# The last group's recurrence in a decoder's third layer: keys read from PSUM, own buffers, four passes on GpSimd, VectorE's order by hand

## The chip, the core and the metric

The kernel runs on one core of a Trainium2 chip. The metric is the device time of one execution in microseconds (us); the median of several runs counts. A core has five engines that each follow a queue of their own: TensorE (PE), VectorE (DVE), ScalarE (ACT), GpSimd (POOL) and SyncE (SP), which here issues the DMA transfers.

## The reference, cut to what matters

A decoder of four layers is computed, each with self-attention, attention to a context and a feed-forward part, with a layer norm after each of them. x is 64 sequences of 64 tokens with 256 channels, in float32. The change lies in the second of the three parts of the third layer, in which the context's rows are the values v and x's own rows are the keys k of a recurrence over the tokens:

```python
def step(carry, kv_t):
    p, q, o = carry
    kt, vt = kv_t
    no = jnp.maximum(o, u + kt)
    A = jnp.exp(o - no)
    E = jnp.exp(u + kt - no)
    y = (A * p + E * vt) / (A * q + E)
    no2 = jnp.maximum(w + o, kt)
    A2 = jnp.exp(w + o - no2)
    E2 = jnp.exp(kt - no2)
    return ((A2 * p + E2 * vt, A2 * q + E2, no2), y)
...
x = _layernorm(x + _L2_xattn_ref(64, 64, 256, L2_xattn_w, L2_xattn_u, x, ctx_2048), axis=-1)
x = _layernorm(x + _L2_ffn_ref(x, L2_ffn_weight, L2_ffn_bias), axis=-1)
```

w and u have one value for each of the 256 channels. The part that follows (`_L2_ffn_ref`) quantizes x to FP8 with one scale for the whole of x, so it needs the largest absolute value of all 64 sequences before it can begin.

## The kernel before

The 4096 tokens are eight groups of 512 (`self.X[g]`, here x0 to x7); all of them stay in SBUF, and so does the context, turned (`self.CT[g]`). `l2_mix` does the self-attention and feed-forward of the third layer and the recurrence. Its feed-forward runs over 64 slots, eight for each group (`hidden`, `down`). Beside the slots of a group stand the parts of the next group's attention (`mixing`) and the parts of the recurrence of the group before (`behind`).

`recurrence(g)` splits the 256 channels into two halves c of 128, which lie on the partitions, with the 512 tokens along the columns. The parts of a half:

- `keys`: x[g] is turned on PE (`turned`, four transposes into a PSUM bank) and ScalarE copies it to the tile `k` (L1458).
- `maximum`: a scan on VectorE gives o (L1574).
- `factors`: two passes on VectorE and a memset fill the first two of the four rows of blocks of the tile e (`es[c]`, named l2x_e0 and l2x_e1 or, without numbers, l2x_e); on ScalarE two Relu passes (L1588, L1589) and one Exp over all 2048 columns (L1590) make the four factors.
- `sums`: the values times two of the factors (`ev`, L1593), and two scans (`pq`, L1599).
- `outputs` (L1602, L1605, L1606) and `divided` (a reciprocal, L1609, and a product, L1610): y.

`finish` turns y back on PE (tile yx, L1621), adds x (L1624), normalizes (`normalized`: statistics on VectorE, L331 and L334; the power -1/2 on GpSimd, L305; four passes on ScalarE, L363) and takes the largest absolute value (`linear.largest`, L60). The two halves share one buffer each of o, pq and ev.

What orders the work: PE's order is that of the program (`manual_schedule`); that of the other engines, and of SP's queue, is made by a scheduler of the language from its own estimates. Each queue is worked off in order.

For the last group no slots are left. PE is given filler instead: `fill(n)` computes n of the 28 units of `ContextRows`, keys and values of the fourth layer for some rows of the context. One unit is two matmuls of 128x512 into a PSUM bank (tag kv, three banks, L168), a copy by ScalarE to a buffer in SBUF (L172, four buffers) and a store to DRAM by SP (L173). The end of `l2_mix`:

```python
fill(2)
self.l3a_qk = [self.big_weight(name) for name in ("l3a_wq", "l3a_wk")]
for k, (_, part) in enumerate(behind):
    if k == len(behind) - 1:
        fill(17)
    part()
```

The tiles e0 and e1 are two of the eight slots of the ring in which weights lie. After the recurrence, `l3_attn` begins with `linear.first` (the FP8 part for x0, with the last seven units) and loads l3a_wv and l3a_wproj (L402), two slots each. The second half of l3a_wv takes e0's slot and the first half of l3a_wproj takes e1's, so these loads wait for the last reader of e0 and e1. ScalarE scales l3a_wproj when it has landed (L2008).

Of the kernel before, what the change touches and what calls it, by code (L numbers as in the profile page):

```python
# [10 lines left out]
F32 = mybir.dt.float32  # L11
# [3 lines left out]
AF = mybir.ActivationFunctionType  # L15
ALU = mybir.AluOpType
# [3 lines left out]
P = 128  # L20
# [3 lines left out]
NTOK = TG * P  # L24
# [7 lines left out]
class Linear:  # L32
# [26 lines left out]
    def largest(self, g):  # L59
        self.nc.vector.tensor_reduce(  # L60
            self.cols[:, g : g + 1], self.dec.X[g], AX.XY, ALU.max, apply_absolute_value=True
        )
# [80 lines left out]
class ContextRows:  # L143
# [16 lines left out]
    def fill(self, n, pool, tag, bufs, banks, copy):  # L160

        dec = self.dec
        while n and self.units:
            n -= 1
            g, t, i = self.units.pop(0)
            ps = dec.bank("kv", bufs=banks)
            for c in range(2):
                dec.nc.tensor.matmul(  # L168
                    ps, dec.CT[g][:, c, t * P : (t + 1) * P], self.w[:, i, c, :], start=c == 0, stop=c == 1
                )  # L170
            out = pool.tile([P, 512], F32, tag=tag, name="kv", bufs=bufs)
            copy(out, ps)  # L172
            dec.nc.sync.dma_start(out=self.dram[g, t, i], in_=out)  # L173
# [97 lines left out]
class Decoder:  # L271
# [1145 lines left out]
    def l2_mix(self, ctx, linear):  # L1417
# [8 lines left out]
        nc, ins = self.nc, self.ins  # L1426
        EPS, HC, NB = 1.1920929e-07, 8, NTOK // S
        wk = self.pool(ctx, "l2m", 2)
# [3 lines left out]
        for c in range(2):  # L1432
            w = self.weight(f"l2_wsg{c}")
# [9 lines left out]
        fill = lambda n: context.fill(n, wk, "hid", 4, 3, nc.scalar.copy)  # L1443
        w, u = self.column("l2_w", 2), self.column("l2_u", 2)
        decay = wk.tile([P, 2, NB, S], F32, tag="decay", name="decay", bufs=1)
# [3 lines left out]
        state = {}  # L1449

        def bank(name):
            return self.bank(name, tag="a", bufs=3)

        def turned(src, out, c):
            ps = bank("tr")
            for t in range(TG):
                nc.tensor.transpose(ps[:, t * P : (t + 1) * P], src[:, t, c * P : (c + 1) * P], self.ident)
            nc.scalar.copy(out, ps)  # L1458

# [94 lines left out]
        def recurrence(g):  # L1556


            x, v = self.X[g], self.CT[g]
            k = wk.tile([P, 2, NTOK], F32, tag="k", name="k", bufs=1)  # L1560
            y = wk.tile([P, 2, NTOK], F32, tag="yx", name="yx", bufs=1)
            halves = []
            for c in range(2):
                e = es[c]
                o = wk.tile([P, NTOK + 1], F32, tag="o", name="o", bufs=1)
                pq = wk.tile([P, 2, NTOK + 1], F32, tag="pq", name="pq", bufs=1)
                ev = wk.tile([P, 2, NTOK], F32, tag="ev", name="ev", bufs=1)

                def keys(c=c):
                    turned(x, k[:, c, :], c)  # L1570

                def maximum(c=c, o=o):
                    nc.gpsimd.memset(o[:, 0:1], NEG_INF)
                    nc.vector.tensor_tensor_scan(  # L1574
                        o[:, 1:], decay[:, c].rearrange("p b t -> p (b t)"), k[:, c, :], 0.0, ALU.add, ALU.max
                    )

                def factors(c=c, o=o, e=e):


                    nc.vector.scalar_tensor_tensor(
                        e[:, 0, :], o[:, :NTOK], u[:, c : c + 1], k[:, c, :], ALU.subtract, ALU.subtract
                    )
                    nc.vector.scalar_tensor_tensor(
                        e[:, 1, :], o[:, :NTOK], w[:, c : c + 1], k[:, c, :], ALU.add, ALU.subtract
                    )
                    nc.vector.memset(e[:, 0:2, :].rearrange("p i (b t) -> p i b t", b=NB)[:, :, :, 0:1], NEG_INF)
                    nc.scalar.activation(e[:, 2:4, :], e[:, 0:2, :], AF.Relu)  # L1588
                    nc.scalar.activation(e[:, 0:2, :], e[:, 0:2, :], AF.Relu, scale=-1.0)  # L1589
                    nc.scalar.activation(e, e, AF.Exp, scale=-1.0)  # L1590

                def sums(c=c, e=e, ev=ev, pq=pq):
                    nc.vector.tensor_tensor(  # L1593
                        ev, e[:, 2:4, :], v[:, c, :].unsqueeze(1).broadcast_to([P, 2, NTOK]), ALU.mult
                    )

                    nc.gpsimd.memset(pq[:, :, 0:1], 0.0)
                    for i, add in enumerate((ev[:, 1, :], e[:, 3, :])):
                        nc.vector.tensor_tensor_scan(pq[:, i, 1:], e[:, 1, :], add, 0.0, ALU.mult, ALU.add)  # L1599

                def outputs(e=e, ev=ev, pq=pq):
                    nc.vector.tensor_tensor(  # L1602
                        pq[:, :, :NTOK], pq[:, :, :NTOK], e[:, 0, :].unsqueeze(1).broadcast_to([P, 2, NTOK]), ALU.mult
                    )
                    nc.vector.tensor_tensor(pq[:, 0, :NTOK], pq[:, 0, :NTOK], ev[:, 0, :], ALU.add)  # L1605
                    nc.vector.tensor_tensor(pq[:, 1, :NTOK], pq[:, 1, :NTOK], e[:, 2, :], ALU.add)  # L1606

                def divided(c=c, pq=pq):
                    nc.vector.reciprocal(pq[:, 1, :NTOK], pq[:, 1, :NTOK])  # L1609
                    nc.vector.tensor_tensor(y[:, c, :], pq[:, 0, :NTOK], pq[:, 1, :NTOK], ALU.mult)  # L1610

                halves.append(([keys], [maximum, factors], [sums, outputs, divided]))

            def finish():
                z = wk.tile([P, TG, D], F32, tag="z", name="z")
                for i in range(2):
                    ps = bank("yx")
                    for j in range(2):
                        for c in range(2):
                            at = (2 * i + j) * P  # L1620
                            nc.tensor.transpose(  # L1621
                                ps[:, j * D + c * P : j * D + (c + 1) * P], y[:, c, at : at + P], self.ident
                            )
                    nc.vector.tensor_tensor(  # L1624
                        z[:, 2 * i : 2 * i + 2, :], ps.rearrange("p (t d) -> p t d", t=2), x[:, 2 * i : 2 * i + 2, :], ALU.add
                    )
                self.normalized(x, z)
                linear.largest(g)

            steps = [part for parts in zip(*halves) for half in parts for part in half]  # L1630
            return steps + [lambda: None, finish]

        def mixing(g):

            def two(t):
                qkv(g, t)
                mixed(g, t - 1)

            return [
                lambda: start(g), lambda: qkv(g, 0), lambda: two(1), lambda: two(2), lambda: two(3),  # L1640
                lambda: mixed(g, 3), lambda: None, lambda: outputs_turned(g),
            ]

        with self.tc.manual_schedule(engines={mybir.EngineType.PE}):
            for part in mixing(0):
                part()
            slots = [(g, i) for g in range(self.n_groups) for i in range(HC)]
            parts, behind, done = [], [], []
            for n in range(len(slots) + 2):
                if n < len(slots):  # L1650
                    g, i = slots[n]
                    if i == 0:
                        parts = mixing(g + 1) if g + 1 < self.n_groups else []
                    hidden(g, i)
                if n >= 2:
                    down(*slots[n - 2])
                    if slots[n - 2][1] == HC - 1:
                        behind += [(n + 2, part) for part in recurrence(slots[n - 2][0])]

                        if slots[n - 2][0] == self.n_groups - 2:  # L1660
                            behind[-1] = (len(slots) + 1, behind[-1][1])
                if n == len(slots) + 1:
                    fill(2)

                for _ in range(2 if n < len(slots) - HC else 3):
                    if behind and n >= behind[0][0]:
                        behind.pop(0)[1]()
                if parts:
                    parts.pop(0)()
            fill(2)  # L1670
            self.l3a_qk = [self.big_weight(name) for name in ("l3a_wq", "l3a_wk")]
            for k, (_, part) in enumerate(behind):
                if k == len(behind) - 1:
                    fill(17)
                part()

    def head_rms(self, wk, ps, out, eps, tag):

# [769 lines left out]
```

## Time and profile before

| | |
|---|---|
| median of 5 runs (lowest to highest) | 4342.58 us (4339.46 to 4348.26) |
| profiled execution: its own time, its span | 4344.71 us, 4343.0 us |
| PE busy | 4081.9 us (94%) |
| VectorE busy | 3093.3 us (71%) |
| ScalarE busy | 2018.8 us (46%) |
| GpSimd busy | 1498.6 us (35%) |
| `l2_mix` and the start of `l3_attn` | about 1354 to 1926 us of the span |
| last group's recurrence, first scan to last product of y | 1871.88 to 1902.52 us |

All times in the text are counted from the start of the span, on one profiled execution. A line such as L1574 is a line of the kernel before; where an operation is in a helper, its line is the helper's. Engines are named as in the profile: PE (matmuls; PEld loads weights beside them), DVE, ACT, POOL, SP. "busy" is the share of the span in which an engine computes; the number in brackets at the end of a timeline's line is the idle time before it and what ended it.

### The profile page before, as it was taken

Reading aid. Unit: us, or ns where it says so; the run is one execution under the profiler, and the core shown is the slowest. Engines: PE = TensorE matmul, PEld = TensorE weight load, DVE = VectorE, ACT = ScalarE, POOL = GpSimd, SP = SyncE. Lnnn points to the kernel's source line nnn. Section 1 sums busy time; section 2 is a strip of 40 time slices with the busy share of each in tenths; the row PEclk is TensorE's granted clock in tenths of the full one; section 3 lists DMA queues with packets and bytes.
Section 4 is the critical chain, followed back from the end, with each engine's and each line's share of the span. In section 5 each row is a group of like instructions: output and inputs, shape, how many; then the busy total and the mean of one; then the engine's idle time right before and its main releaser. Section 6 shows DMA issues by size and latency. Waiting matters only on the chain. (4 is left out here: it accounts for less than half of the span.)

```text
span 4343.0 us, 74101 instructions
## 1 busy us (share of the span) xinstructions
PE 4081.9 (94%) x28808; PEld 2636.8 (61%) x28808; DVE 3093.3 (71%) x6211; ACT 2018.8 (46%) x3695; POOL 1498.6 (35%) x1529
## 2 busy tenths in 40 slices
PE   8889999989988999989999999999989999999898
PEld 6645556666665555546666666666656666666566
DVE  6744548888665687877777777777767778787676
ACT  5555535666523566544444444444432333232443
POOL 4411111332431111115555555555533444433111
PEclk9989998999999999999999999999999999999999
DMA  2200012333200000031111111111130000000000
GB/s 84 66 21 10 1 34 64 76 78 70 73 1 12 1 1 1 10 131 26 29 26 28 28 25 30 25 28 27 30 105 20 20 23 23 23 23 13 9 15 16
DMA packets 108295, 144.01 MB, mean 33 GB/s; under 512 B 15844, under 2 KB 73380, under 8 KB 106536
## 3 DMA queue, kind: packets, MB, share of 16 engines
q1 hardware_dynamic: 107944, 139.27, 12.6%
q8 instruction: 228, 3.74, 0.4%
q14 instruction: 123, 1.01, 0.1%
HBM read 70.25 MB, written 26.76 MB: 22 GB/s over the span
## 5 line engine op out<-in xcount | busy, mean ns | idle before, releaser
L305 POOL TENSOR_TENSOR hrq<-hrq,neg_half 128x4 f32<-128x4 f32 x256 | 258.5, 1010 | 570.9 <-DVE hrq L303 568.5
L305 POOL TENSOR_TENSOR rstd<-rstd,neg_half 128x4 f32<-128x4 f32 (+1 forms) x171 | 149.3, 874 | 706.1 <-DVE rstd L303 638.4
L1188 DVE TENSOR_REDUCE mc<-sq 128x2 f32<-128x512 f32 x512 | 317.6, 683 | 67.5 <-PE sk L1186 66.3
L1194 ACT ACTIVATE e<-sk 128x512 f32<-128x512 f32 x512 | 265.8, 608 | 116.4 <-PE sk L1186 114.5
L1183 PE MATMUL sq<-l1x 32*128 32x256 f32 x2048 | 279.2, 412 | 4.9 <-DVE z L1069 3.1
L1186 PE MATMUL sk<-l1x 32*128 32x256 f32 x2048 | 257.3, 398 | 0.0
L1703 PE MATMUL p<-l3a_wq,xt 128*128 128x512 f32 x512 | 242.1, 595 | 11.2 <-DVE v L292 9.9
L305 POOL TENSOR_TENSOR hrk<-hrk,neg_half 128x4 f32<-128x4 f32 x160 | 188.5, 1178 | 178.3 <-DVE hrk L303 173.7
L1703 PE MATMUL p<-l3a_wk,xt 128*128 128x512 f32 x512 | 247.4, 606 | 0.6 <-ACT q L290 0.6
L1183 PEld LDWEIGHTS sq<-l1x 32*128 32x128 f32 x2048 | 211.6, 198 | 58.8 <-issue 23.2
L1703 PE MATMUL p<-l3x_wq,xt 128*128 128x512 f32 x512 | 242.8, 597 | 0.7 <-DVE k L2087 0.7
L2189 PE MATMUL acc<-l3x_wo,yt 128*128 128x256 f32 x1024 | 235.6, 383 | 2.5 <-ACT yt L290 1.2
L1703 PE MATMUL p<-l3a_wv,xt 128*128 128x512 f32 x512 | 234.0, 599 | 0.4 <-ACT y L94 0.4
L1985 PE MATMUL acc<-l3a_wproj,yt 128*128 128x256 f32 x1024 | 232.7, 380 | 0.2 <-DVE yt L292 0.2
L1985 PEld LDWEIGHTS acc<-l3a_wproj,yt 128*128 128x128 f32 x1024 | 194.6, 191 | 53.6 <-issue 29.2
L2063 ACT ACTIVATE sq<-q 128x512 f32<-128x512 f32 x128 | 80.7, 630 | 311.5 <-DVE q L2087 304.2
L2189 PEld LDWEIGHTS acc<-l3x_wo,yt 128*128 128x128 f32 x1024 | 193.1, 192 | 35.5 <-issue 7.4
L1186 PEld LDWEIGHTS sk<-l1x 32*128 32x128 f32 x2048 | 192.1, 190 | 6.8 <-issue 2.9
L311 PEld LDWEIGHTS qT<-ident,q 128*128 128x128 f32 x1024 | 121.5, 141 | 122.0 <-issue 79.8
L311 PE MATMUL qT<-ident,q 128*128 128x128 f32 x1024 | 158.3, 277 | 26.9 <-DVE qT L292 19.7
L1969 POOL TENSOR_TENSOR hry<-hry,neg_half 128x8 f32<-128x8 f32 x64 | 106.3, 1660 | 183.2 <-DVE hry L1965 183.2
L1222 PE MATMUL ret<-e,vt 128*32 128x256 f32 x2048 | 140.4, 389 | 17.4 <-DVE mc L1188 16.4
(401 smaller groups left out, 10205.9 us busy)
## 6 DMA issues: line engine op xcount, KB each, us to landing
vs<-v SPq DMA_DIRECT2D x320, 128.0 KB
l3x_kv<-kv SPq DMA_DIRECT2D x28, 256.0 KB
x<-in_x SPq DMA_DIRECT2D x8, 512.0 KB
ct<-in_ctxT SPq DMA_DIRECT2D x8, 512.0 KB
cn<-in_ctx SPq DMA_DIRECT2D x8, 512.0 KB
l1x<-in_ctx SPq DMA_DIRECT2D x128, 32.0 KB
l1x_x<-x SPq DMA_DIRECT2D x8, 512.0 KB
l1x<-l1x_x SPq DMA_DIRECT2D x128, 32.0 KB
```

Source lines behind the costliest of these rows:

```text
L305: nc.gpsimd.tensor_tensor(out, out, self.neg_half[:, :n], ALU.pow)
L311: self.nc.tensor.transpose(ps[:, j * P : (j + 1) * P], blk, self.ident)
L1183: nc.tensor.matmul(ps[:, n, :], x_[rows, j, part], c_[rows, j, :], start=True, stop=True)
L1186: nc.tensor.matmul(ps[:, n, :], c_[rows, j, part], x_[rows, j, :], start=True, stop=True)
L1188: nc.vector.tensor_reduce(mc[new % 2][:, ra + k, 2 * j : 2 * j + 2], ps, AX.X, ALU.max, negate=True)
L1194: nc.scalar.activation(es[rb + k], ps, AF.Exp, scale=scale)
L1222: nc.tensor.matmul(ret[32 * r : 32 * r + 32, :], vt[i % 2][:, lc, 4 * r + j, :], es[r][:, lc, :], start=lc == 0, stop=lc == 1,)
L1703: self.nc.tensor.matmul(ps, lhs(c), w(c, cols), start=c == 0, stop=c == 1 and bias is None)
L1969: nc.gpsimd.tensor_tensor(r, r, self.neg_half[:, :8], ALU.pow)
L1985: nc.tensor.matmul(acc[:, :D], yts[h % 2][:, h // 2, :], wp[n // 8][:, (n % 8) * D : (n % 8 + 1) * D], start=n == 0, stop=n == 15,)
L2063: nc.scalar.activation(sq, x, AF.Square)
L2189: nc.tensor.matmul(acc[:, :D], yts[h % 2][:, h // 2, :], w.o[n // 8][:, (n % 8) * D : (n % 8 + 1) * D], start=n == 0, stop=n == 15,)
```

## The change

For the last group alone (`last`):

- The scan and the two passes of `factors` read the turned keys from the PSUM banks, without the copy to `k`. `turned` returns the bank when no tile is given.
- Half 1 has its own buffers for `pq` and `ev`: those of the tags xt and k.
- GpSimd does `ev` of half 1 and the three passes of `outputs` of half 0.
- ScalarE does the Exp in two passes of 1024 columns for each half, that of the last two blocks first.
- At the last slot a one-column Exp is put on ScalarE.
- Where VectorE's order before was the scheduler's, it is the program's from the end of the slots on (`manual_schedule` with DVE): the passes that normalize x6 (`apply`) and its maximum (`largest`) are put between the parts of the last recurrence, and half 1 is divided ahead of half 0.
- Three units of filler stand ahead of x6's transposes and one behind, for two and two; fill(17) stands behind the two halves' factors in the program, which in PE's order is behind the turned keys, as before.

For all groups pq is 512 columns wide, the scans have 511 columns, and of the two sums in `outputs` that of the divisor comes first. GpSimd's and ScalarE's order and SP's queue are still the scheduler's. In the built program SP's queue is changed in two places: the load into e0's slot stands behind the store of the sixth unit (it was the eleventh) and the load into e1's slot behind that of the twelfth (it was the sixteenth); on ScalarE the scaling of the first half of l3a_wproj stands behind the copy of unit 15 (it was the nineteenth).

```diff
@@ turned
             for t in range(TG):
                 nc.tensor.transpose(ps[:, t * P : (t + 1) * P], src[:, t, c * P : (c + 1) * P], self.ident)
+            if out is None:
+                return ps
             nc.scalar.copy(out, ps)
+            return out
@@ recurrence
             x, v = self.X[g], self.CT[g]
-            k = wk.tile([P, 2, NTOK], F32, tag="k", name="k", bufs=1)
+            last = g == self.n_groups - 1
+            ks = {}
+            if not last:
+                k = wk.tile([P, 2, NTOK], F32, tag="k", name="k", bufs=1)
...
-                pq = wk.tile([P, 2, NTOK + 1], F32, tag="pq", name="pq", bufs=1)
-                ev = wk.tile([P, 2, NTOK], F32, tag="ev", name="ev", bufs=1)
+                own = last and c == 1
+                pq = wk.tile([P, 2, NTOK], F32, tag="xt" if own else "pq", name="pq", bufs=2 if own else 1)
+                ev = wk.tile([P, 2, NTOK], F32, tag="k" if own else "ev", name="ev", bufs=1)
 
                 def keys(c=c):
-                    turned(x, k[:, c, :], c)
+                    ks[c] = turned(x, None if last else k[:, c, :], c)
...
                     nc.scalar.activation(e[:, 2:4, :], e[:, 0:2, :], AF.Relu)
+                    if last:
+                        nc.scalar.activation(e[:, 2:4, :], e[:, 2:4, :], AF.Exp, scale=-1.0)
                     nc.scalar.activation(e[:, 0:2, :], e[:, 0:2, :], AF.Relu, scale=-1.0)
-                    nc.scalar.activation(e, e, AF.Exp, scale=-1.0)
+                    rest = e[:, 0:2, :] if last else e
+                    nc.scalar.activation(rest, rest, AF.Exp, scale=-1.0)
 
                 def sums(c=c, e=e, ev=ev, pq=pq):
-                    nc.vector.tensor_tensor(
+                    eng = nc.gpsimd if last and c == 1 else nc.vector
+                    eng.tensor_tensor(
                         ev, e[:, 2:4, :], v[:, c, :].unsqueeze(1).broadcast_to([P, 2, NTOK]), ALU.mult
                     )
...
-                        nc.vector.tensor_tensor_scan(pq[:, i, 1:], e[:, 1, :], add, 0.0, ALU.mult, ALU.add)
+                        nc.vector.tensor_tensor_scan(
+                            pq[:, i, 1:], e[:, 1, : NTOK - 1], add[:, : NTOK - 1], 0.0, ALU.mult, ALU.add
+                        )
...
+                def outputs(c=c, e=e, ev=ev, pq=pq):
+                    eng = nc.gpsimd if last and c == 0 else nc.vector
+                    eng.tensor_tensor(
+                        pq, pq, e[:, 0, :].unsqueeze(1).broadcast_to([P, 2, NTOK]), ALU.mult
                     )
-                    nc.vector.tensor_tensor(pq[:, 0, :NTOK], pq[:, 0, :NTOK], ev[:, 0, :], ALU.add)
-                    nc.vector.tensor_tensor(pq[:, 1, :NTOK], pq[:, 1, :NTOK], e[:, 2, :], ALU.add)
+                    eng.tensor_tensor(pq[:, 1, :], pq[:, 1, :], e[:, 2, :], ALU.add)
+                    eng.tensor_tensor(pq[:, 0, :], pq[:, 0, :], ev[:, 0, :], ALU.add)
...
@@ the end of l2_mix
+                if n == len(slots) - 1:
+                    h = state[slots[n][0], "h", slots[n][1]]
+                    nc.scalar.activation(self.small(1, "none", bufs=1), h[:, 0:1], AF.Exp, scale=0.0)
...
-            fill(2)
+            ended(part for _, part in behind)
+
+        with self.tc.manual_schedule(engines={mybir.EngineType.PE, mybir.EngineType.DVE}):
+            fill(3)
+            statistics, apply, largest = before()
+            statistics()
+            fill(1)
             self.l3a_qk = [self.big_weight(name) for name in ("l3a_wq", "l3a_wk")]
-            for k, (_, part) in enumerate(behind):
-                if k == len(behind) - 1:
-                    fill(17)
-                part()
+            (keys0, keys1, *factors, sums0, outputs0, divided0, sums1, outputs1, divided1), finish = recurrence(
+                self.n_groups - 1
+            )
+            keys0()
+            keys1()
+            ended(factors)
+            fill(17)
+            sums0()
+            outputs0()
+            apply()
+            sums1()
+            outputs1()
+            largest()
+            divided1()
+            divided0()
+            ended(finish())
```

## The prediction

> **What bounds the kernel now.** The page first: PE is busy 94% of the span and its row of 40 slices has no hole, so a change on another engine pays only where PE waits. Then the four engines' timelines from 1820 us, where the last group's recurrence lies. All times are the trace's, in us from the span's start; columns are start, duration, engine, line, what is written from what, count, and in brackets the idle time before and who ended it. PE:
>
> ```profile
> 1868.54 10.46 PE L168 MATMUL kv<-l3x_wkv,ct 128*128 128x512 f32 x24
> 1883.27 20.85 PE L168 MATMUL kv<-l3x_wkv,ct 128*128 128x512 f32 x44 [4.26 <-ACT kv L172]
> 1903.95 1.04 PE L1621 MATMUL yx<-ident,yx 128*128 128x128 f32 x8
> ```
>
> These are the 17 filler units (4 records each). A unit takes 1.72 us (the copies of its result follow each other at 1890.46, 1892.18, 1893.89). Units are numbered here 1 to 28 from the first filler; fill(17) is 5 to 21. The transposes of y stand behind them in PE's order and start at 1903.95. VectorE and ScalarE:
>
> ```profile
> 1871.88 1.22 DVE L1574 TENSOR_TENSOR_SCAN o<-decay,k 128x512 f32<-128x512 f32 x1
> ...
> 1881.83 1.23 DVE L1593 TENSOR_TENSOR ev<-l2x_e,ct 128x1024 f32<-128x1024 f32 x1 [4.34 <-ACT l2x_e L1590]
> ...
> 1887.21 0.69 DVE L1606 TENSOR_TENSOR pq<-pq,l2x_e 128x512 f32<-128x512 f32 x1
> ...
> 1901.83 0.69 DVE L1610 TENSOR_TENSOR yx<-pq 128x512 f32<-128x512 f32 x1
> 1904.59 1.29 DVE L1624 TENSOR_TENSOR z<-yx,x 128x512 f32<-128x512 f32 x2 [2.07 <-PE yx L1621]
> ```
>
> ```profile
> 1878.59 1.28 ACT L1590 ACT_TABLE_LOAD   x1
> ...
> 1905.12 2.00 ACT L2008 ACTIVATE l3a_wproj<-l3a_wproj,l3a_sw 128x2048 f32<-128x2048 f32 x1 [3.77 <-DMA l3a_wproj<-in_l3a_wproj]
> ```
>
> y is ready at 1902.5, yet the transposes wait until PE is through with its filler: **PE ends last here, by 1.4 us, not the recurrence.** PE lost 4.26 us at 1879.0 because unit 11 needs the bank of unit 8, whose copy ScalarE makes only at 1882.65, between its factor passes; and the clock fell behind that gap (the windows view; the granted clock is the third number from the end, 0.55):
>
> ```profile
> 1883.30:1887.00 3.70, 3.70 (x5) 1.59 (x6) 3.63 (x4) 2.98 (x4) 0.00 (x0) 0.55 0.36 137
> ```
>
> The clock's own record has half speed for 3.41 us, so 1.7 us lost. Last, SP, which issues in its order:
>
> ```profile
> 1858.38 29.25 SPq L173 DMA_DIRECT2D l3x_kv<-kv  x11
> 1887.92 0.33 SPq L402 DMA_DIRECT2D l3a_wv<-in_l3a_wv  x1
> 1889.36 7.19 SPq L173 DMA_DIRECT2D l3x_kv<-kv  x5
> 1898.43 0.38 SPq L402 DMA_DIRECT2D l3a_wproj<-in_l3a_wproj  x1
> ```
>
> The second half of l3a_wv takes the ring slot of e0 and is issued 0.02 us after the last reader of e0 (L1606, 1887.21 + 0.69), behind the store of unit 11. l3a_wproj takes e1's slot, behind unit 16.
>
> **The change, part by part.** T is the start of the y transposes, 1903.95 before; everything behind T (z, x7, the maximum, the FP8 product) keeps its order and moves with T.
>
> *Keys from PSUM, x6's pass and maximum moved back.* In the written order x7's statistics close one z-add (0.57) earlier, about 0.4; x7 is written at 1867.5 instead of 1867.89, its first four transposes end 0.4 later, and the scan needs no copy (L1458), no x6 passes (2.08 on ACT) and no maximum (1.22 on DVE): it starts at 1867.9 instead of 1871.88, 4.0 earlier. A pass that reads PSUM is taken at the same price: L1529 with a PSUM operand takes 0.68, L1605 without one 0.69.
>
> *Factors.* DVE's six passes take 5.6 as before (1871.88 to 1877.48), memsets done at 1870.8 and 1873.5. ACT then has eight passes of 1024 columns at 1.06, pitch 0.96 (L1588, L1589), for four of these and two of 2048 before, at the same work in sum; the table load (1.28) is gone from here, since the dummy Exp loads it at 1854, where ACT idles (the 9.44 us in front of 1857.73). e0 complete at 1875.8 (before 1881.8), e1 at 1879.2 (before 1885.0). But unit 6's copy stands behind seven of them, at 1877.65: unit 9 waits for its bank, PE idles 1875.0 to 1878.3, 3.3 instead of 4.26, and I charge the half clock again (1.7). With nothing else in the way, unit 13 ends at 1888.6 and T is 1888.6 + 8 x 1.72 = 1902.4: 1.6 gained.
>
> *GpSimd's four passes.* A two-tensor 128x1024 pass there takes 2.36 (L1268), a 128x512 one 1.27 (L2080). The first needs e1's high half, 1876.8. Side by side with VectorE, e0 would be free at 1876.8 + 2.36 + 2.36 + 1.27 = 1882.8. The trace says that they do not run side by side. GpSimd, then VectorE, at 597 us:
>
> ```profile
> 597.53 2.34 POOL L1039 TENSOR_TENSOR xb<-x,l_bo 128x1024 f32<-128x1024 f32 x1
> ```
>
> ```profile
> 597.60 2.29 DVE L539 SCALAR_TENSOR_TENSOR nmr<-bnmv,rstd 128x4 f32<-128x4 f32 x1 [1.12 <-POOL rstd L305]
> ```
>
> A 128x4 VectorE pass, 0.15 elsewhere, lasts until GpSimd's ends. The other way round, with two scans queued on VectorE:
>
> ```profile
> 1497.28 1.23 DVE L1599 TENSOR_TENSOR_SCAN pq<-l2x_e,ev 128x512 f32<-128x512 f32 x1
> 1498.42 1.20 DVE L1599 TENSOR_TENSOR_SCAN pq<-l2x_e 128x512 f32<-128x512 f32 x1
> ```
>
> ```profile
> 1497.47 1.86 POOL L1471 TENSOR_TENSOR r<-m,neg_half 128x4 f32<-128x4 f32 x1
> ```
>
> GpSimd's 1.04 us pass becomes 1.86: it waits for the first scan and gets in ahead of the end of the second. So I let them alternate: scan 1 of half 0 to 1877.0, GpSimd's ev to 1879.3, scan 2 to 1880.5, scan of half 1 to 1881.7, GpSimd's product to 1884.05, scan to 1885.25, GpSimd's sum to 1886.5. **e0 free at 1886.5**, y ready near 1899.3: VectorE ends 3 us earlier than before and is no bound.
>
> [...]
>
> *What the SP queue makes of it.* In the changed program's order the l3a_wv load stands behind the store of unit 6, not 11, and waits for GpSimd's sum, the last reader of e0. Queued behind it: the stores of units 7 to 10, copied from 1879 on. Who waits: the copy of unit 11 reuses unit 7's buffer, and unit 14 needs unit 11's bank. The landing records give wv 5.6 us from issue (1887.92 to 1893.53) and the next store 0.7 after it (1894.27). So unit 7's store lands at 1886.5 + 5.6 + 0.7 = 1892.8, unit 11 is copied by 1893.4, unit 14 starts there: PE stands 4.8 us, where the trace before never waited for a store. Next, l3a_wproj stands behind unit 12's store (it was 16's) and its scaling (L2008, 2.00) behind unit 15's copy on ACT, where before it came after the last copy. From unit 14's start: issue +0.7, 6.6 to land (1898.43 to 1905.03), scaling done +9.3, unit 16's copy +9.9, which frees the bank for unit 19; three units more, +15.1 instead of 8 x 1.72 = 13.8. T = 1893.4 + 15.1 = 1908.5, +0.4 where the half clock behind the second gap shows: **4.5 to 4.9 later than before.**
>
> *At nothing:* the other seven groups (scans of 511 columns, sums swapped, one memset more) lie under PE, 20.00 of 20 us busy in the windows from 1780 to 1840; if that cover failed, 0.1 a reciprocal, 14 times. The third unit ahead of x6's transposes moves z by 0.3, under statistics already queued. The own buffers of half 1 (those of xt and k) were last read groups earlier: the memset of its pq waits on GpSimd for PE's products of group 6, done before r (L1471) of group 7 in front of it.
>
> **Sum.** Profiled execution 4344.71 + 4.5 = 4349.2; it lies 2.1 above the median, so I predict 4347 for the median. About 0.2% (8.7 us) is what a measurement of this kernel can tell from no change.
>
> **Rivals.** *The passes overlap after all, or the load blocks nothing.* e0 free at 1882.8: T = 1882.8 + 22.4 = 1905.1, +1.1. If moreover the stores do not queue behind the load, 1902.4, and without the half clock 1900.7: -3.3, the best there is, since PE cannot end its filler sooner. For it: wide GpSimd passes beside PSUM-reading VectorE ones keep their time (L1268). Against: the four scans and products read SBUF twice. 28%.
>
> *Slower: VectorE goes first at every handover.* GpSimd's product and sum then follow VectorE's whole half 1, e0 is free at 1889.2, T 1911.7, +7.7; with the load taking wproj's 6.6 instead of 5.6 it is 8.7. It decides from e0 free at 1890.3. For it: VectorE's passes are queued back to back. Against: the 1.86 row. 22%, half of it past 0.2%.
>
> *It doesn't do what it says:* VectorE's order is written out, so GpSimd's ev (not VectorE) may hold half 1 and y end behind PE. It would need y 9 us later than reckoned: 2%, within the slower share.
>
> **How the numbers follow.** Forecast 48% (+3 to +6), the first rival 28% (-3.3 to +1.1), the slower one and the last 24%. Half of the slower one's 22 and the last's 2 lie past 0.2%: slower 0.13. No case gains 8.7; of the first rival's 28 I leave 4 to what I have not seen: faster 0.04, same 0.83. The range takes -3 to +10 about the median.
>
> **What would show it.** Right: the first scan near 1868, no table load behind it, e0's Exp done near 1876; GpSimd passes over 2.36 or VectorE scans stretched; l3a_wv issued at the end of GpSimd's 128x512 sum with PE idle from 1888.6; L2008's scaling ahead of the last copies; T after 1904. Wrong: the transposes before 1902, all GpSimd passes at 2.36 and 1.27 with scans at 1.2, or PE without a gap behind 1880.

## The result and the profile after

The changed kernel takes 4350.15 us (median of 21 runs, 4342.31 to 4358.04) against 4342.58 us: a ratio of 1.0019 with a 95% interval of 1.0013 to 1.0025, so 6 to 11 us slower. The prediction was 4347, with a range from 3 us below the median of before to 10 us above it: direction and place were right, the size was short by 3 us of 8.

The profiled execution took 4355.23 us (span 4353.5), 10.5 more than that of before. Of these 10.5, 3.9 lie before `l2_mix` comes to its first gate product, in code that nothing changed, and that start moved between 1377.8 and 1385.8 us over all the traces of this study; behind the start of l3a 1.1 are given back. So the traces are compared by a stretch: from the first gate product (L1524, now L1527) to the first product of l3a. It took 544.4 us before and takes 552.2 after, 7.8 more, close to the 7.6 between the medians. In its parts, with T the start of the y transposes and unit 5 the first behind the turned keys (a time given as "behind unit 5" counts from its start):

| | before | after | difference | predicted |
|---|---|---|---|---|
| first gate product to x7's transposes | 484.54 | 482.99 | -1.55 | -0.4 |
| x7's transposes to unit 5 | 2.07 | 2.33 | +0.26 | 0 |
| unit 5 to T | 35.41 | 42.39 | +6.98 | +4.9 to +5.3 |
| T to the first product of l3a | 22.35 | 24.46 | +2.11 | 0 |

PE's timeline after; the columns are those of the lines of before:

```profile
1868.78 0.33 PE L1457 MATMUL tr<-ident,x 128*128 128x128 f32 x1 [2.09 <-ACT x L363]
...
1871.11 8.47 PE L168 MATMUL kv<-l3x_wkv,ct 128*128 128x512 f32 x16
...
1882.40 8.85 PE L168 MATMUL kv<-l3x_wkv,ct 128*128 128x512 f32 x20 [2.82 <-ACT kv L172]
...
1897.63 16.04 PE L168 MATMUL kv<-l3x_wkv,ct 128*128 128x512 f32 x32 [6.38 <-ACT kv L172]
...
1913.50 1.04 PE L1636 MATMUL yx<-ident,yx 128*128 128x128 f32 x8
...
1921.69 7.11 PE L168 MATMUL kv<-l3x_wkv,ct 128*128 128x512 f32 x12 [2.28 <-ACT kv L172]
```

Read it by the brackets. Unit 9 waits 2.82 us for unit 6's copy, unit 14 waits 6.38 us (before, no gap stood there), T is 1913.50, and behind T unit 24 waits 2.28 us where before it was 1.86. The second number shows the clock: 20 matmuls at 0.43 us take 8.6 (the line's 8.85 runs to the end of the last one), and the 16 from unit 5 on take 8.47 instead of 6.9. The windows view gives the granted clock, third number from the end, for the first 3.4 us from unit 5, unit 9, unit 14 and unit 24 on:

```profile
1871.10:1874.50 3.40, 3.40 (x7) 1.55 (x6) 3.31 (x5) 0.00 (x0) 0.52 (x2) 0.57 0.20 77
1882.40:1885.80 3.40, 3.40 (x8) 1.62 (x9) 3.40 (x4) 3.04 (x6) 2.18 (x2) 1.00 0.21 80
1897.63:1901.00 3.37, 3.37 (x4) 1.49 (x5) 3.33 (x3) 1.07 (x2) 0.00 (x0) 0.50 0.66 186
1921.70:1925.10 3.40, 3.40 (x4) 1.43 (x5) 3.31 (x21) 0.42 (x1) 0.02 (x1) 0.51 0.41 154
```

Half speed behind the idle time of 2.09 in front of x7's transposes, behind the 6.38 and behind the 2.28; full speed behind the 2.82. GpSimd and VectorE:

```profile
1881.01 2.38 POOL L1605 TENSOR_TENSOR ev<-l2x_e,ct 128x1024 f32<-128x1024 f32 x1 [7.57 <-ACT l2x_e L1598]
1884.62 3.19 POOL L1617 TENSOR_TENSOR pq<-pq,l2x_e 128x1024 f32<-128x1024 f32 x1 [1.22 <-DVE nmr L361]
1887.88 2.06 POOL L1620 TENSOR_TENSOR pq<-pq,l2x_e 128x512 f32<-128x512 f32 x1
1889.90 2.24 POOL L1621 TENSOR_TENSOR pq<-pq,ev 128x512 f32<-128x512 f32 x1
```

```profile
1870.62 1.22 DVE L1582 TENSOR_TENSOR_SCAN o<-decay,tr 128x512 f32<-128x512 f32 x1 [0.19 <-PE tr L1457]
...
1881.16 3.31 DVE L1611 TENSOR_TENSOR_SCAN pq<-l2x_e 128x511 f32<-128x511 f32 x1
...
1885.58 3.30 DVE L1611 TENSOR_TENSOR_SCAN pq<-l2x_e 128x511 f32<-128x511 f32 x1
...
1901.78 0.69 DVE L1625 TENSOR_TENSOR yx<-pq 128x512 f32<-128x512 f32 x1
```

The scan starts without a copy and costs 1.22 from PSUM as from SBUF. In these rows GpSimd's passes and VectorE's scans take turns: scans of 1.20 last 3.31 and 3.30 (their wait counted in) and end 1.1 us behind the end of GpSimd's ev (1883.39) and of its product (1887.81); GpSimd's product lasts 3.19, its sums 2.06 and 2.24, where the prediction had 2.36 and 1.27. Two scans follow each other only where GpSimd's product still waits for the first of them (to 1884.47). y is ready at 1902.47, 11 us ahead of T. What these passes hold back is seen on SP and ScalarE:

```profile
1889.97 0.33 SPq L402 DMA_DIRECT2D l3a_wv<-in_l3a_wv  x1
1890.39 8.46 SPq L173 DMA_DIRECT2D l3x_kv<-kv  x6
1898.95 0.55 SPq L402 DMA_DIRECT2D l3a_wproj<-in_l3a_wproj  x1
```

```profile
1896.99 0.59 ACT L172 COPY kv<-kv 128x512 f32<-128x512 f32 x1 [9.33 <-DMA l3x_kv<-kv]
...
1905.72 2.00 ACT L2047 ACTIVATE l3a_wproj<-l3a_wproj,l3a_sw 128x2048 f32<-128x2048 f32 x1 [1.92 <-DMA l3a_wproj<-in_l3a_wproj]
```

The load of l3a_wv goes out 0.03 after GpSimd's sum (1887.88 + 2.06), the stores behind it. The landing records give 1896.24 for the load and 1896.89 for unit 7's store, and 0.10 later ScalarE copies unit 11, after 9.33 us of idleness that the profile puts down to a store. l3a_wproj lands at 1905.62 and its scaling goes ahead of three filler copies. PE's line shows no gap for that: with half speed behind the 6.38 (0.50 in the view above), PE comes to unit 19 at about 1908.2, just when the first of the three copies, unit 16's, is done (it starts at 1907.63 and takes some 0.6). This second stall stands behind the first and does not add to it.

### The profile page after: what moved, and what is told of

It reads as the page before. It is cut to its first block, busy times and chain, and to the rows that moved or that the text cites. A ratio compares the mean times of both kernels' runs of the same rounds, so it can differ in the third digit from the quotient of the medians.

```text
span 4353.5 us, 74103 instructions
## 1 busy us (share of the span) xinstructions
PE 4087.7 (94%) x28808; PEld 2637.0 (61%) x28808; DVE 3095.8 (71%) x6207; ACT 2018.7 (46%) x3696; POOL 1508.6 (35%) x1533
```

## The experiments

Theory A was that of the prediction: the cost comes from *when e0 and e1 are let go* and from what stands behind their loads on SP and behind the scaling on ScalarE. Its rivals: GpSimd's passes cost time of themselves; PE's half clock is the loss; a wrong place of the filler units is. The code cuts are shortened. All kernels, with the stretch of their traces and their times (ratio to the kernel before, run beside them):

| kernel | unit 5 to T | T to l3a | stretch | median, us | ratio [95%] |
|---|---|---|---|---|---|
| before | 35.4 | 22.4 | 544.4 | 4342.6 | |
| after | 42.4 | 24.5 | 552.2 | 4350.2 | 1.0019 [1.0013, 1.0025] |
| all passes on VectorE | 37.4 | 23.2 | 545.6 | 4342.3 | 0.9999 [0.9990, 1.0008] |
| only half 1's ev on GpSimd | 38.8 | 24.5 | 548.3 | 4347.0 | 1.0008 [0.9999, 1.0016] |
| eight copy buffers | 42.6 | 24.4 | 552.1 | 4348.6 | 1.0010 [1.0002, 1.0019] |
| eight buffers, scaling on GpSimd | 34.4 | 24.5 | 544.3 | 4341.0 | 0.9992 [0.9984, 1.0001] |
| SP's order written | 33.8 | 25.8 | 544.7 | 4343.4 | 1.0003 [0.9994, 1.0012] |
| two units ahead | 41.6 | 24.5 | 552.1 | 4350.5 | 1.0019 [1.0010, 1.0028] |
| aggregates one pass later | 43.9 | 22.3 | 551.6 | 4351.6 | 1.0013 [1.0004, 1.0022] |
| the best version | 29.7* | 22.4 | 537.2 | 4336.2 | 0.9983 [0.9974, 0.9992] |
| the best version, GpSimd's passes back | 35.5* | 22.3 | 542.7 | 4339.5 | 0.9996 [0.9987, 1.0005] |

\* from unit 6, since one unit more stands ahead.

### All passes on VectorE

```diff
-eng = nc.gpsimd if last and c == 1 else nc.vector
+eng = nc.vector
...
-eng = nc.gpsimd if last and c == 0 else nc.vector
+eng = nc.vector
```

> The changed kernel with its four GpSimd passes (ev of half 1, the product and the two sums of half 0) given back to VectorE; orders of ScalarE and SP stay as they are. Theory A (the last reader of e0 holds the l3a_wv load, the load holds the stores of units 7 to 10 on SP, the store of unit 7 holds the copy of unit 11, that holds unit 14): in the changed kernel's frame VectorE reads e0 for the last time near 1884.3 instead of 1889.9, unit 7's store lands near 1891, before unit 11 itself is through, so the 6.38 us gap in front of unit 14 goes; T near 1906.5 instead of 1913.5, the time 7 us (0.16%) below the changed kernel and within 0.05% of the kernel before. Rival B (the loss is the half clock of PE behind its gaps, whatever makes them): the gap in front of unit 9 and its half clock stay, so no more than the half clock behind the second gap comes back, 2 us. Rival C (the passes overlap usefully and VectorE is short of time): y comes later than T and the kernel gets slower than the changed one.

```profile
1874.15 8.85 PE L168 MATMUL kv<-l3x_wkv,ct 128*128 128x512 f32 x20 [2.81 <-ACT kv L172]
1884.00 8.85 PE L168 MATMUL kv<-l3x_wkv,ct 128*128 128x512 f32 x20 [1.00 <-ACT kv L172]
1894.93 5.42 PE L168 MATMUL kv<-l3x_wkv,ct 128*128 128x512 f32 x12 [2.08 <-ACT kv L172]
```

The 6.38 in front of unit 14 is 1.00, the stretch falls by 6.6 and the time is that of the kernel before. e0 was free at 1876.08, which is 13.3 behind unit 5 (after: 18.8). With the orders of SP and ScalarE as they are in the changed program, the four passes are the cause of the loss. T came back by 5.0 and not 7, because 1.00 is left (ScalarE still waits for a store) and 2.08 now stand in front of unit 19 (the scaling). Rival B falls: the 2.81 in front of unit 9 stayed, and 6.6 us came back where it allowed 2. So does rival C: y was ready 8.2 us ahead of T.

### Only half 1's ev on GpSimd

```diff
-eng = nc.gpsimd if last and c == 0 else nc.vector   # outputs
+eng = nc.vector
```

> The changed kernel with only the outputs of half 0 (product and two sums) given back to VectorE; GpSimd keeps the product ev of half 1. Theory A: e0's last reader is VectorE's sum, near 1886.5 instead of 1889.9 (the first scan pair is still split by GpSimd's ev, one lock of 2.3 us instead of four), so unit 14 starts 3.4 earlier, the gap in front of it is 3.0 instead of 6.4, T 3.4 earlier and the time 3 to 4 us below the changed kernel, half way to the kernel before. Rival B (half clock): as the changed kernel within 1 us, since both gaps stay over 2.5 us. Rival C (VectorE short of time): slower than the changed kernel.

The load of l3a_wv was issued 15.5 behind unit 5, 3.4 earlier than after, as expected; the gap in front of unit 14 was 2.08 (expected 3.0; 0.53 stood in front of unit 12), T 3.6 earlier. The median is 3.2 lower, but the intervals of the two kernels overlap. By the traces the cost is about in proportion: one GpSimd pass (beside it a scan of 3.31) frees e0 2.1 us later than none and makes the stretch 2.7 longer; the four passes together do 5.5 and 6.6.

### Eight copy buffers

```diff
-fill = lambda n: context.fill(n, wk, "hid", 4, 3, nc.scalar.copy)
+fill = lambda n: context.fill(n, more, "hid", 4, 3, nc.scalar.copy)   # last part: 4 of hid, 4 halves of yt
```

> The changed kernel with eight buffers instead of four for the filler units' copies in its last part (four more out of the idle tiles of yt); GpSimd's passes, the SP order and the ScalarE order stay. Theory A: the l3a_wv load is still issued near 1889.9 and the stores of 7 to 10 still behind it, but unit 11's copy no longer needs unit 7's buffer, so the 6.38 us gap in front of unit 14 goes. What then ends last is the second stall: l3a_wproj issued near 1894.5, landed near 1901, scaled to 1903, the copy of unit 16 behind it, so unit 19 waits 1 to 2 us; T 1907 to 1909 instead of 1913.5 and the time 4 to 6 us below the changed kernel. Rival B (GpSimd's lock itself costs the time, by a late y): nothing comes back, since y and the passes are as they were. Rival C (the landing of the load is what PE waits for in another way): the gap stays.

PE, and ScalarE's scaling:

```profile
1874.19 17.73 PE L168 MATMUL kv<-l3x_wkv,ct 128*128 128x512 f32 x40 [2.77 <-ACT kv L172]
1897.28 8.45 PE L168 MATMUL kv<-l3x_wkv,ct 128*128 128x512 f32 x12 [5.37 <-ACT kv L172]
```

```profile
1894.75 2.00 ACT L2060 ACTIVATE l3a_wproj<-l3a_wproj,l3a_sw 128x2048 f32<-128x2048 f32 x1 [4.88 <-DMA l3a_wproj<-in_l3a_wproj]
```

The gap in front of unit 14 is gone, and T is no earlier: 5.37 stand in front of unit 19 instead. My 4 to 6 us were wrong. l3a_wproj took 8.8 us to land (issued 1885.88, landed 1894.65), not 6.6, and the three units to T took 8.45 behind the new gap, where with all passes on VectorE they took 5.42 behind 2.08; I put the difference down to the clock, an estimate. Taking one of two stalls in series away moved the wait to the other. Rival B had forecast that nothing comes back, but not for this reason: y was ready 11.3 us ahead of T.

### Eight buffers, and l3a_wproj's first half scaled by GpSimd

```diff
-nc.scalar.activation(wp[i], wp[i], AF.Copy, scale=sw)
+if i == 0:
+    nc.gpsimd.tensor_scalar(wp[i], wp[i], sw, None, ALU.mult)
+else:
+    nc.scalar.activation(wp[i], wp[i], AF.Copy, scale=sw)
```

> The kernel with eight copy buffers, and beside that the first half of l3a_wproj scaled by GpSimd instead of ScalarE, so that no filler copy stands behind the scaling; GpSimd's four passes stay. Measured so far, from the mixer's first gate product to the first product of l3a: before 544.4, changed kernel 552.2, eight buffers 552.1 (there the gap in front of unit 14 was gone and 5.37 stood in front of unit 19, behind the scaling). Theory A (two stalls in series, both made by the order on SP and ScalarE and not by GpSimd's passes as such; with one gone the other takes its place): the gap in front of unit 19 goes too, from unit 5 to T 35.3 instead of 42.6, this stretch 545, the time 6 to 8 us below the changed kernel and within 0.05% of the kernel before, with the passes on GpSimd where they were. Rival B (GpSimd's passes cost the time by themselves): y ends last and T stays above 40 from unit 5. Rival C (PE waits for the transfers in any case): the stretch stays near 552.

```profile
1877.83 15.72 PE L168 MATMUL kv<-l3x_wkv,ct 128*128 128x512 f32 x36 [2.78 <-ACT kv L172]
1893.93 7.13 PE L168 MATMUL kv<-l3x_wkv,ct 128*128 128x512 f32 x16 [0.38 <-ACT kv L172]
```

```profile
1885.33 2.25 POOL L1621 TENSOR_TENSOR pq<-pq,ev 128x512 f32<-128x512 f32 x1
...
1898.84 5.46 POOL L2061 TENSOR_SCALAR l3a_wproj<-l3a_wproj,l3a_sw 128x2048 f32<-128x2048 f32 x1 [11.26 <-DMA l3a_wproj<-in_l3a_wproj]
```

GpSimd's four passes are where they were, as long as they were, and both stalls are gone: from unit 5 to T 34.4 us, the stretch 544.3, 7.9 less than after. This decides against "the passes cost time of themselves": with the copies freed from SP's stores and from the scaling, the passes can have cost PE no more than the 0.38 in front of unit 18; the 2.78 in front of unit 9 stands there without them too (2.81).

### SP's order written out

```diff
-with self.tc.manual_schedule(engines={PE, DVE}):
+with self.tc.manual_schedule(engines={PE, DVE, SP}):
```

> The changed kernel with SP's order written out too in the last group's part: the loads of l3a_wv now stand behind the stores of units 12 and 15 (was unit 6), that of l3a_wproj behind unit 18 (was 12), and ScalarE's scaling of l3a_wproj behind the copy of unit 21 (was 15). Four copy buffers, GpSimd's four passes and VectorE's order stay. Theory A (the loads' place in the queue makes both stalls): no gap in front of unit 14 and none in front of unit 19; from unit 5 to T 34 to 35.5 instead of 42.4, from the first gate product to the first product of l3a 543.5 to 546 instead of 552.2, the time 6 to 8 us below the changed kernel. Rival B (the four buffers stall somewhere in any order, since a store behind a 1 MB load lands 6 us late): the gap in front of unit 14 reappears in front of unit 17 or 20 with 3 to 5 us, and 2 to 4 us come back. Rival C (the scaling, now next to x7's passes, holds x7): T is early, but from T to the first product of l3a it takes 2 to 4 us more than 24.4.

```profile
1881.61 22.58 PE L168 MATMUL kv<-l3x_wkv,ct 128*128 128x512 f32 x52 [2.81 <-ACT kv L172]
...
1913.59 7.11 PE L168 MATMUL kv<-l3x_wkv,ct 128*128 128x512 f32 x12 [3.65 <-ACT kv L172]
```

52 matmuls stand without a gap from unit 9 to T, with four buffers and GpSimd's passes untouched: the new order takes the two stalls away, 33.8 us from unit 5 to T. It moved more than one thing, so what each is worth is not shown: the loads of l3a_wq, l3a_wk and the first half of l3a_wv went back in the queue too (they had stood ahead of unit 1's store), and on ScalarE the scaling now stands behind unit 21's copy, where it can't hold T. Together with the first experiment it says that the loss needs both, GpSimd's late release and this place of the loads and the scaling: without either the stretch is near that of before (545.6 and 544.7). Rival B's gap did not come. Rival C was right in kind: l3a_wproj now lands at 1908.99, its scaling stands in front of x7's passes, and unit 24 waits 3.65. T came 8.6 earlier from unit 5, and 1.4 of it was given back behind T, where rival C had 2 to 4.

### Two filler units ahead of x6's transposes

```diff
-fill(3)
+fill(2)
 ...
-fill(1)
+fill(2)
```

> The changed kernel with two filler units ahead of x6's transposes and two behind them, as in the kernel before, instead of three and one. Theory A: the idle of 2.09 us in front of x7's transposes shrinks below 1.5, no half clock behind it, unit 5 ends 1.6 earlier, its copy and the first relu with it; e0's factors, e0's release and T come 1.2 to 1.6 earlier: the time 1 to 2 us below the changed kernel. Rival B (the half clock behind the gaps is the main loss): the same here, but with T 2 to 4 earlier, since the gap in front of unit 14 shrinks too. Rival C (the placement costs nothing): T as in the changed kernel.

Nothing moved: 1.0019, the stretch 552.1. PE's idle time in front of x7's transposes was 1.33 and not 2.09, but x7 came 0.4 later, the clock still showed 0.70 from unit 5 on and 0.71 from unit 9 on, and T lay at the same distance from the first gate product to 0.1. The place of the unit is not where the time went, as rival C had it.

### Aggregates one pass later

```diff
 for t in range(n_tiles):
     nc.vector.bn_stats(...)   # tile t
-    nc.vector.bn_aggr(...)    # tile t
+    nc.vector.bn_aggr(...)    # tile t - 1
```

> The changed kernel with x7's second statistics in the other order: the aggregate of each row tile one statistics pass later, as the kernel before had it. Theory A (VectorE's written order puts each aggregate right behind its own statistics pass, four pitches of 0.53 instead of 0.39 us, so x7 comes 0.5 us later, the gap in front of unit 24 is 2.28 instead of 1.86 and the clock halves behind it): gap 1.8 to 1.9, the three units behind it 5.4 instead of 7.1 us, from T to the first product of l3a 22.3 instead of 24.4, the time 2 us (0.05%) below the changed kernel. Rival B (the gap and the half clock there have another cause): 24.4 as before.

```profile
1906.49 5.42 PE L168 MATMUL kv<-l3x_wkv,ct 128*128 128x512 f32 x12 [1.41 <-ACT kv L172]
...
1919.46 5.42 PE L168 MATMUL kv<-l3x_wkv,ct 128*128 128x512 f32 x12 [1.81 <-ACT kv L172]
```

The lines are as expected: unit 24 waits 1.81, the units behind it take 5.42 instead of 7.11, and T to l3a is 22.3. Of the 2.1 us, some 0.5 is the shorter gap and 1.7 the clock. Behind the 1.81 the granted clock was 1.00, behind the 2.28 of after 0.51. That it stays up because the gap is shorter is not shown: with all passes on VectorE it was 1.00 behind 2.33. The time does not show the gain: in this execution T came 1.5 later, since l3a_wproj took 8.2 us to land (6.7 after) and unit 19 waited 1.41 for its scaling. By time inconclusive; by this trace 2.1 us behind T.

### A version that beats both

All passes on VectorE; eight buffers; `fill(3)` and `fill(2)` around x6's statistics; the aggregates one pass later; and ScalarE's order written out in this part:

```diff
+with self.tc.manual_schedule(engines={PE, DVE, ACT}):
+    fill(1); maximum0(); factors0()      # four ScalarE passes of half 0
+    fill(2); maximum1(); high1()         # two of half 1
+    fill(1); low1(); fill(2)             # the other two
+    sums0(); outputs0(); fill(1); apply(); fill(9)
+    sums1(); outputs1(); largest(); divided1(); divided0()
```

> A version that tries to beat both: all passes on VectorE, eight copy buffers, three filler units ahead of x6's transposes and two behind them, the aggregates one pass later, and ScalarE's order written out as well in this part, so that the copies of units 6, 7 and 8 (by the new count) go between the factor passes and not behind them. Theory A (PE's gaps and the half clock behind each are all that lies between the kernel and its 1.72 us a unit): no gap over 1 us from unit 6 to T, T 27.5 to 29 behind unit 6, the stretch from the first gate product to the first product of l3a 535 to 538 instead of 544.4 in the kernel before, the time 6 to 9 us (0.15 to 0.2%) below the kernel before. Rival B (with the filler faster y ends last): PE waits in front of T for 1 to 3 us and the clock halves behind it, gain 3 to 5 us. Rival C (the scaling of l3a_wproj stalls unit 21 again): a gap in front of T, gain under 3 us.

```profile
1870.33 7.03 PE L168 MATMUL kv<-l3x_wkv,ct 128*128 128x512 f32 x16
1877.66 19.53 PE L168 MATMUL kv<-l3x_wkv,ct 128*128 128x512 f32 x44 [0.29 <-ACT kv L172]
1898.24 1.98 PE L168 MATMUL kv<-l3x_wkv,ct 128*128 128x512 f32 x4 [1.04 <-ACT kv L172]
```

16 units in 29.7 us where 27.5 (16 of 1.72) is the least, just outside the 27.5 to 29 of theory A; the stretch (537.2) and the time are inside its bounds. y was ready 2.6 ahead of T, so rival B did not come, and of rival C 1.04 us remain. 4336.2 us: 0.9983 [0.9974, 0.9992], about 7 us below the kernel before; the changed one, in runs of its own, was 0.19% above it. Five things changed at once here, and their shares are not shown.

### The same with GpSimd's passes

```diff
-eng = nc.vector
+eng = nc.gpsimd if last and c == 1 else nc.vector   # and outputs of half 0
```

> The version that beat both kernels (4336.2; eight buffers, ScalarE's order written, one more filler unit ahead), with GpSimd's four passes put back as the change has them. Theory A (the passes cost by releasing e0 and e1 late, not by their own time): e0 free 5 us later than without them, the load of l3a_wv and with it the landing of l3a_wproj and its scaling later, the gap in front of the last units 3 to 5 us instead of 1.0; T 31.5 to 34.5 behind the first unit after x7's transposes instead of 29.7, the stretch from the first gate product to the first product of l3a 539 to 542 instead of 537.2, the time 2 to 5 us above that version and still 2 to 5 us below the kernel before. Rival B (with the stalls covered the passes cost nothing): 537 and the same time. Rival C (the passes take load from VectorE and y comes earlier): under 536.

GpSimd, VectorE's next scan, and PE:

```profile
1874.45 2.36 POOL L1629 TENSOR_TENSOR pq<-pq,l2x_e 128x1024 f32<-128x1024 f32 x1 [6.75 <-DVE nmr L366]
1876.89 1.27 POOL L1632 TENSOR_TENSOR pq<-pq,l2x_e 128x512 f32<-128x512 f32 x1
1878.11 1.26 POOL L1633 TENSOR_TENSOR pq<-pq,ev 128x512 f32<-128x512 f32 x1
1879.34 2.35 POOL L1617 TENSOR_TENSOR ev<-l2x_e,ct 128x1024 f32<-128x1024 f32 x1
```

```profile
1881.72 1.22 DVE L1623 TENSOR_TENSOR_SCAN pq<-l2x_e,ev 128x511 f32<-128x511 f32 x1 [7.39 <-POOL ev L1617]
```

```profile
1895.39 5.40 PE L168 MATMUL kv<-l3x_wkv,ct 128*128 128x512 f32 x8 [5.15 <-ACT kv L172]
```

Here the passes run undisturbed (2.36, 1.27, 1.26, 2.35), because VectorE has nothing to do: it waits 7.39 us for the last of them, ev of half 1, which stands behind the three others in GpSimd's queue (in the changed kernel it stood first). So theory A had the size, but not the path: e0 is free 1.9 us later than without the passes, not 5, and it is e1 that is late. e1 is free 20.9 us behind unit 6 instead of 17.4, l3a_wproj is issued 0.06 later, and its scaling, now one copy earlier in ScalarE's order, holds unit 20 for 5.15; how much of this is the later load and how much the copy's place is not shown. Stretch 542.7, 5.5 more than without the passes and just above the 539 to 542 expected; the median 3.4 more, with intervals that overlap. So the passes keep their undisturbed times in this version, and by the trace the passes cost nearly as much (5.5 against 6.6), again through a weight load. Against the kernel before, the 2 to 5 us that were expected cannot be told from nothing.

## Why the prediction was right, and where it was short

*Keys from PSUM, factors.* Right in price: scan 1.22, passes 0.75. The chain up to x7's transposes gained 1.5, not 0.4. In the factors a step was left out: behind the 2.09 us in front of x7's transposes the clock was 0.57 over the first 3.4 us of unit 5 and the next, unit 5's copy stands ahead of the first Relu on ScalarE, and e0's last Exp ends 8.9 behind unit 5 and not 7.7. The half clock charged behind unit 9's gap was not there (1.00). The wait in front of unit 9 was charged with 3.3 and measured 2.82.

*GpSimd's passes.* e0 was free 18.8 behind unit 5; the prediction's 1886.5 is 18.4. That they lie so close is partly luck: the chain began 1.2 later (the 8.9) and, from e0's last Exp to e0's release, took 9.95 instead of 10.7. The order of turns that it reckoned from two rows is what happened. "Passes overlap" is refuted by the row of 3.19 beside the 2.36 of the same pass undisturbed. y came 31.4 behind unit 5; predicted 31.2.

*What the SP queue makes of it.* Right link by link: load, stores, unit 7's buffer, unit 11's copy, unit 14. The load's landing, 6.3 and not 5.6, and the later release put unit 14 at 26.5 behind unit 5 instead of 25.3. From unit 14 to T it took 15.9, predicted 15.1 to 15.5. The stall by the scaling, which the prediction has there, is not seen as a gap: half speed behind the 6.38 (0.50 over 3.37 us) costs the same units 1.7 us and brings PE to unit 19 only when unit 16's copy is done. Two small slips change nothing: 1882.8 + 22.4 is 1905.2 and not 1905.1, and before, the scaling stood behind unit 19's copy and not behind the last one.

*"Everything behind T ... moves with T."* **This step failed**, by 2.1 us of the 7.8. VectorE's written order puts each aggregate behind its own statistics pass, a pitch of 0.53 instead of 0.39 us, x7 comes 0.4 later, and the gap in front of unit 24 grows from 1.86 to 2.28, behind which the clock was 0.51 here and 1.00 before: 0.4 of the 2.1 is the gap, 1.7 the clock (7.11 for three units instead of 5.42). The 0.4 was in the change (VectorE's order) and was not looked for behind T. The 1.7 does not follow from the gap's length alone: with all passes on VectorE, in the same order, the clock was 1.00 behind a gap of 2.33. With the 2.0 too little between unit 5 and T and 0.3 more in x7's transposes, less the 1.15 gained ahead of x7 that was not reckoned, it makes the step from 4.5 to 7.8.

*The rivals.* The 28% for overlap fell on the trace; "VectorE first at every handover" fell too (GpSimd gets in behind the first, the third and the fourth scan, not behind VectorE's whole half 1), though its total of 7.7 us is near what was measured, by other terms. The last rival, that y ends behind PE, fell: y was ready 11 us ahead of T.

## What to carry to other kernels

When a pass moves to a slower engine (the product took 1.23 on VectorE before and 2.36 on GpSimd undisturbed), ask who reads its input last and what is waiting to overwrite that input: here a weight load took over the buffer, and in SP's queue it held stores that had nothing to do with it (the load was issued at 1889.97, the next store at 1890.39). Before expecting a gain from removing one wait, cost the next one in the same chain; of two stalls in series the first removal returned nothing (552.1 us against 552.2), both together returned all (544.3, before 544.4). And where an order is written by hand, write it for the short instructions too.

## What the runs showed of the hardware that was not expected

- **The clock and short gaps.** Behind an idle time of PE of 2.28 us in after the granted clock was 0.51 and three units took 7.11 us, where 5.42 is usual; behind 2.26 to 2.30 in four experiments three units took 7.04 to 7.11 too. Behind 2.33 (all passes on VectorE) they took 5.42, and behind the 2.8 in front of unit 9 a matmul took 0.43 us in seven traces of eight (the eighth is two units ahead). The granted clock over the 3.35 to 3.43 us from the end of the gap:

  | gap, us | granted clock behind it |
  |---|---|
  | after, unit 24: 2.28 | 0.51 |
  | all passes on VectorE, unit 24: 2.33 | 1.00 |
  | all passes on VectorE, unit 19: 2.08 | 1.00 |
  | after, unit 9: 2.82 | 1.00 |
  | two units ahead, unit 9: 2.81 | 0.71 |
  | aggregates one pass later, unit 24: 1.81 | 1.00 |

  So the length of the gap alone did not decide: 2.28 was followed by 0.51, 2.33 by 1.00. What did is not shown. In the trace's clock record of after, half speed lasts 3.41 us from 1870.58, 6.83 from 1894.48 and 3.41 from 1921.78; half of 3.41 is the 1.7 us that such a stretch cost behind the 2.28.
- **GpSimd beside VectorE.** In after, with both queues full, the two took turns, and scans took part: 1.20 became 3.31 and 3.30, VectorE's product 2.11 instead of 1.23; GpSimd's product took 3.19 and its sums 2.06 and 2.24, where with VectorE idle they took 2.36, 1.27 and 1.26 (the best version, GpSimd's passes back).
- **Landing of a 1 MB load among stores** took 5.6 to 8.9 us from its issue (l3a_wv 5.6 before, 6.3 after; l3a_wproj 6.6 before, 6.7 after, 8.2 with the aggregates later, 8.8 with eight buffers, 8.9 with SP's order written): a scatter of the size of the effects that were looked for.
- **Scaling 128x2048** took 5.46 on GpSimd and 2.00 on ScalarE; with eight buffers the kernel was faster with the slower one, since no filler copy stood behind it.
